# Two-layer graph network on one NeuronCore: the range guard's products on GpSimd, its largest values in one VectorE reduction

## The chip, the cores and the metric

The kernel runs on one NeuronCore of one Trainium2 chip. The core has five engines that work side by side and wait for each other by semaphores: TensorE (PE in the profile, with its weight loads as PEld), VectorE (DVE), ScalarE (ACT), GpSimd (POOL) and SyncE (SP), which here only issues transfers. The metric is the device time of one execution in microseconds, as the median of five runs.

## The reference

The reference takes 3327 nodes with 64 features and a 0/1 adjacency matrix `adj` of 3327 x 3327, and applies two layers, each with a layer norm and a relu ahead of it and a residual sum behind it.

```
h = max(layernorm(x), 0)
x = x + L0(h, adj)          # hyperbolic graph attention
h = max(layernorm(x), 0)
x = x + L1(h, adj)          # sum over the last 100 neighbours, with decay

L0: c = 1/r**2
    att[i,j] = sigmoid(left[i] + right[j] + b) * adj[i,j]
    support[i] = sum_j att[i,j] * logmap(h[i], h[j], c)
    return proj(expmap(h, support, c), c)

L1: rank = cumsum(adj != 0, axis=1)
    w[i,j] = mask * 0.5**(number of later neighbours of i behind j), for the last 100
    return w @ (h @ weight) + bias
```

`logmap` contains an artanh of a distance that depends on both nodes, so it has to be evaluated for each of the 3327 x 3327 pairs. The kernel's fast version replaces that function of the pair by a fit made of two Gelu evaluations, which is good only while the largest feature norms lie in a certain range. A range guard finds the largest values of three per-node quantities and sets a flag; if the flag is set, a slow general version runs after the fast one. With the inputs of this case it does not.

## The kernel before

Nodes are padded to 26 blocks of 128. The 26 blocks j lie on the partitions in turn, and the nodes i lie along the free axis in four strips of 8, 8, 6 and 4 blocks (`STRIPS`). A round handles one block j (two in the last strip) against one strip: 26 + 26 + 26 + 13 = 91 rounds, numbered n from 0. Each round has the same steps, on tiles of 128 x 1024 (128 x 768 in the third strip):

- SyncE loads a part of the adjacency into `ad` (L616), four rounds ahead of its use, into one of five buffers.
- VectorE turns it into a 0/1 `mask` (L622, `edges`), two rounds ahead.
- TensorE counts the later neighbours into PSUM (L633, L634), and ScalarE or VectorE in turn writes the counts to SBUF (L656 and L660 or L658, `read`). They are kept in `behind_lo`, `behind_hi` and `weight_of` for the second layer.
- TensorE makes the pair distance `pq` (L688, L689, `products`), in one of two PSUM buffers.
- ScalarE evaluates the tanh of the attention into `sg` (L671, `sigmoids`), and two Gelus on `pq`, one after the other in place (L881, `gelu`).
- VectorE forms `(tanh + 1) * ad` (L676, `pair_one`) and `(pq + WD) * sg` (L681, `pair_two`).
- TensorE sums over j (L701, `total`).

Around the rounds lie a set-up (layer norm, the per-node scalars `x2`, `bal`, `nrm` and others from L736 to L802 on VectorE, features in L805 on VectorE and from L820 on ScalarE, transposes on TensorE), and after each strip a stage of small per-node steps (`post`), which runs inside the next strip's rounds, mostly on GpSimd. After the last strip, the second layer multiplies the kept counts' weights with the features (L1269) and transposes back (L1429).

For TensorE, VectorE and ScalarE the program's text fixes the order of instructions (`manual_schedule` with `IN_ORDER`). GpSimd and SyncE are not in that set: the framework's scheduler orders what is issued on them by when it can run, so an instruction can stand in their queues far ahead of where the text has it. On GpSimd the set-up puts, among others, a copy of `x2` (the first strip's `dots`, L1078), `ih` (L963), six DMAs that turn `iu` and `iz` into parts of `ju` and `jz` (L867), the products `hw` (L919), and `su` and `sv` (L964, L965).

The change touches the guard's first part, `range_steps` (L978 to L990). It reads `nrm`, `x2`, `bal` and the constant `node` (0 for padding nodes), all 128 x 26, and writes the four columns of `st`: the largest `nrm`, the largest `c * x2 * nrm`, the largest `bal`, and the largest of `-bal`. It is a generator: `advance` runs it piece by piece between the steps of rounds, and each `yield` names the size of the piece. `PORTIONS[0] = 2` allows two units in each round of the first strip, and the first call of `advance` is in round n = 4, so the four pieces with `yield 2` between them run in the rounds n = 4, 5, 6 and 7, which are the fifth to the eighth. In each, they stand on VectorE right after L681. The guard's second part (`in_range`, L992 to L1009) reads `st` near the end of the rounds.

`post_pool`, where the guard's work tile lies, is allocated in SBUF ahead of the pools `strip` and `work`, whose tiles follow it.

Of the kernel before, what the change touches and what calls it, by code (L numbers as in the profile page):

```python
# [12 lines left out]
F32 = mybir.dt.float32  # L13
# [6 lines left out]
ALU = mybir.AluOpType  # L20
AX = mybir.AxisListType
PSUM = bass.MemoryType.PSUM

P = 128
N = 3327
NB = 26
# [13 lines left out]
BIG, LATER, ACT, POOL = 4, 99, 100, 101  # L40
# [408 lines left out]
def fast(ctx, tc, x, adj_t, r, w_att, b_att, weight, bias, out, flag):  # L449

    nc = tc.nc
    V, A, G, T = nc.vector, nc.scalar, nc.gpsimd, nc.tensor
# [47 lines left out]
    node = const.tile([P, NB], F32, name="node")  # L500
# [4 lines left out]
    def scalar_col(name):  # L505
        return const.tile([P, 1], F32, name=name)

    inv_r, c_c, sqc, absr, maxnorm, c2_c, m2c, p2c, negc, zs_c, za_c, f_c = (
        scalar_col(n) for n in ("inv_r", "c_c", "sqc", "absr", "maxnorm", "c2_c", "m2c", "p2c", "negc", "zs_c", "za_c",
                                "f_c"))  # L510
# [15 lines left out]
    def wide(t, n):  # L526
# [3 lines left out]
    x2, bal, balm, nrm, left, right, sv, su, sk, ih = (  # L530
        const.tile([P, NB], F32, name=n)
        for n in ("x2", "bal", "balm", "nrm", "left", "right", "sv", "su", "sk", "ih"))
# [10 lines left out]
    post_pool = ctx.enter_context(tc.tile_pool(name="post", bufs=1))  # L543
    st = const.tile([P, 4], F32, name="st")
# [431 lines left out]


    def range_steps():  # L978
        t1 = post_pool.tile([P, NB], F32, name="st1")
        V.tensor_mul(t1, nrm, node)  # L980
        V.tensor_reduce(st[:, 0:1], t1, AX.X, ALU.max)
        yield 2
        V.scalar_tensor_tensor(t1, x2, c_c, t1, op0=ALU.mult, op1=ALU.mult)
        V.tensor_reduce(st[:, 1:2], t1, AX.X, ALU.max)
        yield 2
        V.tensor_mul(t1, bal, node)
        V.tensor_reduce(st[:, 2:3], t1, AX.X, ALU.max)
        yield 2
        V.tensor_reduce(st[:, 3:4], t1, AX.X, ALU.min)
        V.tensor_scalar(st[:, 3:4], st[:, 3:4], -1.0, None, op0=ALU.mult)  # L990

    def in_range():  # L992
        pf = ps.tile([P, P], F32, name="pc")
# [270 lines left out]
    def add(j, wt, n):  # L1264
# [5 lines left out]
                 start=j == order[0], stop=j == NB - 1)  # L1270

    stages, rest_of_ahead = [Stage(range_steps())], last_of_ahead()
    range_end = in_range()
    load(LOADS)
# [225 lines left out]
```

## Time and profile before

| | us |
|---|---|
| median of 5 runs | 398.43 (397.96 to 399.12) |
| the profiled execution | 397.54 |
| its span, from the first instruction to the last | 395.8 |
| set-up, until ScalarE's row of L656 at 43.34 | 43.3 |
| rounds of the strips one to three | 43.3 to 288 |
| last strip, last `post`, second layer, output | 288 to 395.8 |

The granted TensorE clock has a mean of 0.992 in this execution. In 40 equal slices, of 9.9 us each (busy share in tenths, 9 for 90% or more), two engines and GpSimd read:

```
DVE  4999999999999999999999999999998999798941
ACT  3589999999999999999999999999988899697510
POOL 8145200000000166842133674951246678234100
```

In the timeline each line has the start in us, the duration in us (of all, where several are merged as "x2"), the engine, the line in the kernel, the operation, the tiles written and read with their shapes, and in brackets the idle time of the engine ahead of it with what ended it. A list of waits has the waiting instruction, the one that released it, and the sum, the number and the longest of these waits. Buffer numbers are left out of tile names, and some names are cut at a digit: the guard's `st1` appears as `st`, `x2` as `x`, `q0_c` as `q_c`. The chain of waits is followed back from the last instruction: at each step to what released it, or to the instruction ahead of it on its engine.

### The profile page before, as it was taken

What the parts mean: (1) busy time and instruction counts of PE and PEld (TensorE: products, weight loads), DVE (VectorE), ACT (ScalarE), POOL (GpSimd) and SP (SyncE); (2) the same over time, 40 slices, a digit from 0 to 9 for tenths busy, and PEclk for the clock granted to TensorE, in tenths of its full rate; (3) what the DMA queues carried; (4) which work ended last, traced back from release to release, by engine and by line L of the source; (5) the groups of instructions that cost most, each with busy time, mean ns of one, the idle gap of its engine ahead of it and who ended that gap; (6) DMA issues with size and microseconds to landing.
All of it is one profiled execution on the core that took longest, in us unless ns stands there. A gap on an engine that the chain in (4) does not pass through costs nothing.

```text
span 395.8 us, 4776 instructions
## 1 busy us (share of the span) xinstructions
PE 350.1 (88%) x1460; PEld 149.3 (38%) x1460; DVE 363.6 (92%) x551; ACT 348.5 (88%) x401; POOL 143.1 (36%) x279
## 2 busy tenths in 40 slices
PE   0077999999999899999998999999987899999892
PEld 0053333333333333333333344444433333344362
DVE  4999999999999999999999999999998999798941
ACT  3589999999999999999999999999988899697510
POOL 8145200000000166842133674951246678234100
PEclk9999999999999999999999999999999999999996
DMA  7314554454557445545444445554654330000022
GB/s 205 153 43 135 174 155 147 132 159 153 159 159 221 130 148 159 159 135 162 133 129 135 132 140 161 144 142 154 189 155 133 109 106 0 2 0 1 2 48 48
DMA packets 23299, 49.00 MB, mean 124 GB/s; under 512 B 8789, under 2 KB 9245, under 8 KB 23265
## 3 DMA queue, kind: packets, MB, share of 16 engines
q1 hardware_dynamic: 20993, 47.66, 39.8%
q10 hardware_dynamic: 1808, 0.46, 0.7%
q0 software_dynamic: 464, 0.49, 0.5%
q8 instruction: 13, 0.21, 0.2%
q14 instruction: 21, 0.17, 0.1%
HBM read 46.40 MB, written 0.87 MB: 119 GB/s over the span
## 4 chain that ended last, share of the span: by engine, by line
DVE 42%; ACT 27%; issue 15%; PE 12%; POOL 2%; DMA 1%; POOLq 0%; DVEq 0%; ACTq 0%
DVE sg L681 12%; DVE sg L676 12%; ACT pq L881 10%; ACT sg L671 7%; PE po L701 4%; DVE mask L622 3%; ACT behind_hi L656 2%; ACT behind_lo L656 2%; DVE behind_hi L660 1%; PE pc L633 1%; DMA x_sb<-in_x 1%; DVE behind_lo L660 1%; PE pc L634 1%; PE pw L1269 1%; PE pw L1429 1%
## 5 line engine op out<-in xcount | busy, mean ns | idle before, releaser
L881 ACT ACTIVATE pq<-pq 128x1024 f32<-128x1024 f32 (+1 forms) x182 | 174.2, 963 | 2.6 <-PE pq L689 0.8
L701 PE MATMUL po<-sg,hw 128*65 128x512 f32 (+1 forms) x364 | 159.6, 562 | 0.1
L681 DVE SCALAR_TENSOR_TENSOR sg<-pq,sg 128x1024 f32<-128x1024 f32 (+1 forms) x91 | 103.6, 1138 | 3.1 <-ACT pq L881 2.4
L676 DVE SCALAR_TENSOR_TENSOR sg<-sg,ad 128x1024 f32<-128x1024 f32 (+1 forms) x91 | 104.8, 1152 | 0.1
L671 ACT ACTIVATE sg<-left_b,right 128x1024 f32<-128x1024 f32 (+2 forms) x103 | 102.0, 991 | 0.0
L701 PEld LDWEIGHTS po<-sg,hw 128*65 128x65 f32 x364 | 48.9, 137 | 67.1 <-issue 52.9
L633 PE MATMUL pc<-mask,ca 128*128 128x512 bf16 (+1 forms) x175 | 63.5, 363 | 8.4 <-ACT behind_hi L656 4.1
L688 PE MATMUL pq<-iu,ju 71*128 71x512 f16 (+1 forms) x182 | 66.5, 366 | 1.1 <-ACT jz L818 0.8
L634 PE MATMUL pc<-mask,cb 128*128 128x512 bf16 (+1 forms) x182 | 64.6, 365 | 1.7 <-DVE mask L622 1.0
L689 PE MATMUL pq<-iz,jz 128*128 128x512 f16 (+1 forms) x182 | 65.0, 364 | 0.0
L622 DVE TENSOR_SCALAR mask<-ad 128x1024 bf16<-128x1024 f32 (+1 forms) x91 | 59.1, 650 | 0.0
L634 PEld LDWEIGHTS <-cb 128*128 128x128 bf16 x182 | 17.7, 97 | 47.1 <-issue 34.3
L1108 POOL CAST w<-mask 128x1 f32<-128x1 bf16 x3 | 1.5, 504 | 89.3 <-ACT sg L671 89.2
L633 PEld LDWEIGHTS <-ca 128*128 128x128 bf16 x175 | 17.1, 98 | 30.5 <-issue 18.3
L688 PEld LDWEIGHTS <-ju 71*128 71x128 f16 x182 | 17.8, 98 | 23.1 <-DVE sg L681 5.5
L1269 PEld LDWEIGHTS <-s 128*128 128x128 f16 x182 | 17.7, 98 | 21.3 <-DVE s L1093 2.3
L689 PEld LDWEIGHTS <-jz 128*128 128x128 f16 x182 | 17.9, 98 | 18.6 <-issue 1.1
L660 DVE TENSOR_SCALAR behind_lo<-pc 128x1024 uint8<-128x1024 f32 (+2 forms) x24 | 24.4, 1017 | 0.3 <-PE pc L634 0.3
L656 ACT ACTIVATE behind_hi<-pc 128x1024 uint8<-128x1024 f32 (+2 forms) x25 | 21.9, 874 | 1.3 <-PE pc L634 1.3
L656 ACT ACTIVATE behind_lo<-pc 128x1024 uint8<-128x1024 f32 (+2 forms) x24 | 20.9, 871 | 0.0
L852 PE MATMUL pq<-id,nui 128*71 128x128 f16 x8 | 1.0, 311 | 20.9 <-ACT nzi L826 20.9
L660 DVE TENSOR_SCALAR behind_hi<-pc 128x1024 uint8<-128x1024 f32 (+2 forms) x15 | 14.8, 985 | 0.9 <-PE pc L634 0.7
(344 smaller groups left out, 382.4 us busy)
## 6 DMA issues: line engine op xcount, KB each, us to landing
ad<-in_adj_t SPq DMA_DIRECT2D x65, 512.0 KB, 3.5
ad<-in_adj_t SPq DMA_DIRECT2D x26, 384.0 KB, 3.1
out<-o SPq DMA_DIRECT2D x6, 128.0 KB, 1.9
left_b<-left_d SPq DMA_DIRECT2D x1, 512.0 KB, 4.2
x_sb<-in_x SPq DMA_DIRECT2D x1, 416.0 KB, 4.8
x_sb<-in_x ACTq DMA_DIRECT2D x1, 416.0 KB
left_b<-left_d SPq DMA_DIRECT2D x1, 384.0 KB
jz<-iz POOLq DMA_DIRECT2D x2, 128.0 KB, 2.6
```

Of the source, the lines that this page charges most:

```text
L622: V.tensor_scalar(*args, 0.0, None, op0=ALU.not_equal)
L633: T.matmul(S.pc[:, f0:f1], ca, S.before[:, f0:f1], start=False, stop=True, skip_group_check=True)
L634: T.matmul(S.pc[:, f0:f1], cb, now[:, f0:f1], start=S.first, stop=True, skip_group_check=True)
L656: A.activation(kept, of, AF.Relu, scale=128.0 if j in JD else 1.0)
L660: V.tensor_scalar(kept, S.pc[:, : S.F], 0.0, None, op0=ALU.max)
L671: A.activation(part(n, sg, j), S.left[:, : S.F], AF.Tanh, bias=right[:, j : j + 1], scale=0.5)
L676: V.scalar_tensor_tensor(sg, sg, 1.0, ad_of.pop(n)[:, :w], op0=ALU.add, op1=ALU.mult)
L681: V.scalar_tensor_tensor(sg, pq_of.pop(n)[:, :w], WD, sg, op0=ALU.add, op1=ALU.mult)
L688: T.matmul(part(n, pq, j, f0, f1), ju[:KB, j, :], S.iu[:, f0:f1], start=True, stop=False)
L689: T.matmul(part(n, pq, j, f0, f1), jz[:, j, :], S.iz[:, f0:f1], start=False, stop=True)
L701: T.matmul(po[: D + 1, : f1 - f0], hw[:, j, :], part(n, sg_of[n], j, f0, f1), start=j == NB - 1, stop=j == 0)
L881: A.activation(pq, pq, AF.Gelu, scale=scale)
```

## The change

The four pieces become two. The first issues five instructions on GpSimd, which write the four products into the four rows of one tile `tops` (128 x 4 x 26): `nrm * node`, `c * x2` times that row, `bal * node`, and minus that row. The second is one VectorE reduction over the last axis, which writes all four columns of `st` at once. `yield LATER` ends a round's share, so in the text the products stand in the round n = 4 and the reduction in n = 5. Eight VectorE instructions become one, and GpSimd gets five more. The work tile grows from 104 to 416 bytes per partition, and in the built program the tiles that lie behind it in `post_pool`, `strip` and `work` move by 288 bytes per partition. The last column was the least `bal` times -1, and is now the largest of `-bal`, which is the same number.

```
     def range_steps():
-        t1 = post_pool.tile([P, NB], F32, name="st1")
-        V.tensor_mul(t1, nrm, node)
-        V.tensor_reduce(st[:, 0:1], t1, AX.X, ALU.max)
-        yield 2
-        V.scalar_tensor_tensor(t1, x2, c_c, t1, op0=ALU.mult, op1=ALU.mult)
-        V.tensor_reduce(st[:, 1:2], t1, AX.X, ALU.max)
-        yield 2
-        V.tensor_mul(t1, bal, node)
-        V.tensor_reduce(st[:, 2:3], t1, AX.X, ALU.max)
-        yield 2
-        V.tensor_reduce(st[:, 3:4], t1, AX.X, ALU.min)
-        V.tensor_scalar(st[:, 3:4], st[:, 3:4], -1.0, None, op0=ALU.mult)
+        tops = post_pool.tile([P, 4, NB], F32, name="tops")
+        G.tensor_mul(tops[:, 0], nrm, node)
+        G.tensor_scalar(tops[:, 1], x2, c_c, None, op0=ALU.mult)
+        G.tensor_mul(tops[:, 1], tops[:, 1], tops[:, 0])
+        G.tensor_mul(tops[:, 2], bal, node)
+        G.tensor_scalar(tops[:, 3], tops[:, 2], -1.0, None, op0=ALU.mult)
+        yield LATER
+        V.tensor_reduce(st, tops, AX.X, ALU.max)
+        yield LATER
```

## The prediction, made before the result was known

> **What bounds the kernel now.** I read the page first (busy shares, then the chain), then the busy time by stage, then ScalarE's waits, then the timeline of VectorE and ScalarE around the steps that the change removes. On the page VectorE is the busiest engine and has the largest share of the chain:
>
> ```profile
> PE 350.1 (88%) x1460; PEld 149.3 (38%) x1460; DVE 363.6 (92%) x551; ACT 348.5 (88%) x401; POOL 143.1 (36%) x279
> DVE 42%; ACT 27%; issue 15%; PE 12%; POOL 2%; DMA 1%; POOLq 0%; DVEq 0%; ACTq 0%
> ```
>
> So work taken from VectorE looks like time won. By stage the answer is closer (columns: stretch, its length, then busy time of PE, PEld, DVE, ACT, POOL; the three rows are the strips one, two and three):
>
> ```profile
> 43.34:127.50 84.16, 83.24 (x286) 31.28 (x285) 83.35 (x93) 83.40 (x86) 1.77 (x2) 1.00 0.53 161
> 127.50:213.00 85.50, 84.11 (x297) 32.20 (x296) 84.83 (x89) 84.74 (x90) 36.10 (x68) 1.00 0.48 147
> 213.00:288.00 75.00, 71.56 (x321) 33.40 (x320) 73.89 (x99) 74.80 (x103) 38.71 (x74) 1.00 0.51 150
> ```
>
> VectorE and ScalarE are both full. What remains of ScalarE's time is 0.03 us ahead of each second L881, which rewrites the first one's tile. Which of the two sets the pace is shown by who waits. ScalarE's waits from 44 to 288 us are one entry, and that is the one that ends at 43.34:
>
> ```profile
> ACT behind_hi L656 <- PE pc L634: 0.3, 1, 0.3
> ```
>
> For 245 us ScalarE waits for nobody, and nothing taken from VectorE inside that stretch can bring a ScalarE instruction forward. The timeline shows where VectorE stands behind it:
>
> ```profile
> 49.55 1.22 DVE L681 SCALAR_TENSOR_TENSOR sg<-pq,sg 128x1024 f32<-128x1024 f32 x1
> 50.68 0.18 DVE L980 TENSOR_TENSOR st<-nrm,node 128x26 f32<-128x26 f32 x1
> 50.90 0.18 DVE L981 TENSOR_REDUCE st<-st 128x1 f32<-128x26 f32 x1
> 50.99 1.22 DVE L676 SCALAR_TENSOR_TENSOR sg<-sg,ad 128x1024 f32<-128x1024 f32 x1
> ...
> 71.95 2.06 ACT L881 ACTIVATE pq<-pq 128x1024 f32<-128x1024 f32 x2
> 75.41 1.21 DVE L681 SCALAR_TENSOR_TENSOR sg<-pq,sg 128x1024 f32<-128x1024 f32 x1
> ...
> 150.34 2.06 ACT L881 ACTIVATE pq<-pq 128x1024 f32<-128x1024 f32 x2
> 152.78 1.22 DVE L681 SCALAR_TENSOR_TENSOR sg<-pq,sg 128x1024 f32<-128x1024 f32 x1
> ```
>
> Take the distance from the end of a round's second L881 to the start of its L681. Before the small steps, L881 ends at 47.27 + 2.05 = 49.32 and L681 starts at 49.55: 0.23. After them it is 75.41 - 74.01 = 1.40. At 152.78 it is 0.38 (150.34 + 2.06 = 152.40), and in the next round, where L881 ends at 155.41 and L681 starts at 155.64, 0.23 again. VectorE falls about a microsecond behind because of the small steps, makes it up by about 150 us, and no instruction of ScalarE shows either. That memory ends there; whatever the small steps did is gone 245 us before the end.
>
> **The removed steps.** VectorE's cost is read from start to start, since its instructions overlap. Without small steps L676 starts 1.13 after L681 (46.68 to 47.81). With them: 50.99 - 49.55 = 1.44, 55.36 - 53.86 = 1.50, 58.53 - 57.10 = 1.43, 62.81 - 61.40 = 1.41. The excess is 0.31 + 0.37 + 0.30 + 0.28 = 1.26 us over four rounds.
>
> **The one reduction added.** No row has 128x104. Bounds: 0.18 (128x26, L981) and four of them, 0.72. Between L981 and L743 (128x832, 1.02 us) the slope is 0.84 / 806 = 1.04 ns per element, so 0.18 + 78 x 1.04 ns = 0.26 us, which I take. VectorE saves about 1.26 - 0.26 = 1.0 us (0.5 to 1.1). On the path to the end I count 0: ScalarE's own row covers it. If that cover were missing, the gain would be 1.0.
>
> **The wait added.** The reduction waits for GpSimd. Behind it stand L676 of round 6 and everything after on VectorE. In the built program's order the five products do not stand where they are written, about 50 us in. They go to the front of GpSimd's queue, between and after the two instructions that the set-up has there, as soon as x2, bal and nrm exist, and ahead of the six DMAs of L867:
>
> ```profile
> 17.51 0.19 POOL L1078 COPY dots<-x 128x8 f32<-128x8 f32 x1 [1.53 <-DVE x L792]
> 18.04 0.32 POOL L963 TENSOR_SCALAR ih<-babs 128x26 f32<-128x26 f32 x1 [0.34 <-DVE babs L796]
> 24.29 0.60 POOL L867 DMA_DIRECT2D ju<-iu  x1 [5.93 <-DVE yr L872]
> ```
>
> Prices: three products of two tiles at 0.24 (L964, 128x26) and two by a constant at 0.32 (L963): 1.36, about 1.6 us with the 0.3 from start to start that L964 and L965 show. GpSimd is then done near 20, against 24.29 for the first DMA: 4 us of the 5.93 idle remain. The reduction stands near 54 and never waits. Cost 0; the DMAs of L867 would be late only if the products took over four times their rows.
>
> **What the products do to VectorE's set-up.** This is the one place where the path is touched. From 17.03 to 18.72 the chain of waits runs through VectorE's L790 to L801 and then to ScalarE's first L820. What is lost there arrives at the end in full. Rows on both sides: from 15.19 to 15.97 GpSimd runs four single-column instructions without a break (L967 to L970), and VectorE's two-operand steps beside them keep their time (L519 0.21, L521 0.23, against 0.21 alone at 16.29 and 16.54). Against that, a large one:
>
> ```profile
> 134.59 1.28 POOL L1109 TENSOR_TENSOR w<-hw,agg 128x512 f32<-128x512 f32 x1
> 135.30 1.65 DVE L676 SCALAR_TENSOR_TENSOR sg<-sg,ad 128x1024 f32<-128x1024 f32 x1
> ```
>
> 1.65 instead of 1.21: 0.44 lost beside 1.28. Our tiles have 26 columns, nearer to one column than to 512. By the small rows the loss is 0 to 0.02 for each of five products, and I take 0.1 in all. The upper bound: L796, L797 and L800, the three two-operand steps of the chain after x2, are each held for one whole product of 0.32, 0.96 us. Below nothing it can't go: nothing on the chain is removed there. Products that fall after 18.8 meet L805, whose reader L825 starts on ScalarE at 19.81 behind four instructions of its own, so a few tenths there are free.
>
> [...]
>
> **SyncE.** The products also shift the load order near 120 us: the third strip's left_b (L583), which today waits 4.3 us for ScalarE in the queue, goes behind that strip's iu loads, and one load of ad behind two iz loads and one iu load. The ad load issued at 121.86 is first read by the mask at 133.56, and loads there land in at most 5.8 us: 5.9 spare. The earlier one, at 120.08, is read at 128.63: 2.8 spare, and it loses the wait ahead of it. left_b is read at 215. Cost 0.
>
> **Sum.** The profiled execution took 397.54 (span 395.8, 1.7 around it). 397.54 + 0 (VectorE) + 0 (wait) + 0.1 (set-up) + 0 (loads) = 397.64. The profile lies 0.89 below the runs' median of 398.43, so on the runs' scale 398.5.
>
> **The rivals.**
> Saving arrives (faster): VectorE is what sets the pace, and 1.0 us reaches the end: 397.4. For it: 92%, 42% of the chain, and the chain does run through VectorE from 46.68 to 69.8. Against it: the chain changes to ScalarE at 70, where ScalarE had already been without a gap since 43.34. 12%.
> GpSimd in VectorE's way (slower): during 17.5 to 18.7 the products hold the chain's steps; at the bound 399.4. It decides from about 0.8 us. For it: L676 at 135.30. Against it: the rows at 15.2 to 16. 15%.
> A load too late (slower): through the new order, or because the larger tile moves all work tiles behind it in SBUF and loads get slower. A load would have to take 2.8 us more than 5.8; then ScalarE's reading of counts would stall, about 1 us: 399.4. 3%.
> The change not doing what it says, with products late and the reduction waiting: it needs GpSimd to be 34 us later than I place it. Within the rest.
>
> **How the numbers follow.** A measurement here tells from no change about 0.2%, 0.8 us. Forecast, no change: 70%, of which 1% each strays over a bound by measurement alone. Faster 0.12 + 0.01 = 0.13; slower 0.15 + 0.03 + 0.01 = 0.19; same 0.68. Range: from 397.5, next to the saving in full, to 399.4, the bound on the set-up.
>
> **What would show it.** Right: five GpSimd rows between 17.5 and 20; VectorE's L681 after 62 us 0.2 to 0.4 behind L881 instead of 1.4; ScalarE's waits from 44 to 288 empty as before; the first L820 within 0.1 of 18.77. Wrong: an L820 at 19.2 or later, a wait of ScalarE on VectorE or PE in strip one, or a mask that waits for a load.

## The result, and the profile after

The change is slower, by about 1.1 us: 399.61 us as the median of 27 runs (398.38 to 401.29) against 398.50 us for 51 runs of the kernel before beside it, ratio 1.0032 with a 95% interval of 1.0021 to 1.0043. The predicted time was 398.5 us and the range ended at 399.4. The profiled execution took 399.36 us against 397.54, its span is 397.6 us against 395.8.

The medians hide how the runs lie. Those of the change fall into two groups, 14 between 398.38 and 399.61 and 13 between 400.44 and 401.29, with nothing between. The kernel before has most of its runs below 399.7 and 8 of 51 above. Below, "lower runs" are those under 399.7 us and "upper runs" the rest. The line was drawn with the runs in view, and three of the change's later runs fall just above it, between 399.7 and 400.0. With the repeats of both kernels:

| | runs | median | mean of the lower runs | upper runs | mean of the upper runs |
|---|---|---|---|---|---|
| before | 224 | 398.56 | 398.45 | 46 (21%) | 400.12 |
| the change | 49 | 399.67 | 399.01 | 24 (49%) | 400.78 |

So there are two things to explain: 0.55 us in the lower runs, and a share of upper runs that is more than doubled. (A kernel that is slower throughout also gets more runs over a fixed line; but 21 of the 49, or 43%, lie even above a line that is 0.55 us higher.)

The profile after shows first that what was predicted of the engines came about. The page has 7 VectorE instructions fewer, 5 more of GpSimd, and the chain lies less on VectorE:

```profile
PE 352.2 (89%) x1460; PEld 151.5 (38%) x1460; DVE 363.6 (91%) x544; ACT 348.4 (88%) x401; POOL 145.4 (37%) x284
...
PE 30%; DVE 29%; ACT 24%; issue 11%; POOL 2%; DMA 2%; POOLq 0%; SPq 0%; DVEq 0%; ACTq 0%
```

The timeline of the change (start, duration, engine, line, operation, tiles) has the five products early in the set-up and the reduction in the round n = 5; line numbers behind the edit are three lower than before:

```profile
17.40 0.43 POOL L981 TENSOR_SCALAR tops<-x,c_c 128x26 f32<-128x26 f32 x1 [1.57 <-DVE yr L793]
...
17.93 0.25 POOL L983 TENSOR_TENSOR tops<-bal,node 128x26 f32<-128x26 f32 x1
...
18.27 0.33 POOL L984 TENSOR_SCALAR tops<-tops 128x26 f32<-128x26 f32 x1
...
18.63 0.32 ACT L820 ACTIVATE g<-g,one_c 128x27 f32<-128x27 f32 x1 [4.39 <-POOL tops L984]
...
18.68 0.80 POOL L963 TENSOR_SCALAR ih<-babs 128x26 f32<-128x26 f32 x1
...
19.44 0.23 POOL L980 TENSOR_TENSOR tops<-nrm,node 128x26 f32<-128x26 f32 x1
...
19.75 0.32 POOL L982 TENSOR_TENSOR tops<-tops 128x26 f32<-128x26 f32 x1
...
20.59 0.18 DVE L839 COPY nui<-nu 128x24 f16<-128x24 f16 x1
...
24.25 0.61 POOL L867 DMA_DIRECT2D ju<-iu  x1 [4.19 <-DVE yr L872]
...
55.25 0.25 DVE L986 TENSOR_REDUCE st<-tops 128x4 f32<-128x104 f32 x1
...
72.45 2.06 ACT L881 ACTIVATE pq<-pq 128x1024 f32<-128x1024 f32 x2
...
74.89 1.22 DVE L681 SCALAR_TENSOR_TENSOR sg<-pq,sg 128x1024 f32<-128x1024 f32 x1
```

The profile puts the release of L820 down to L984, but L820 doesn't read `tops`; it starts 1.74 us behind the start of L790, as it did before. L881 ends at 74.51 and L681 starts at 74.89: 0.38 us behind, where it stood 1.40 behind before. VectorE's saving is there. ScalarE's waits from 44 us to 289 us, however, are the same single entry as before, with the same 0.3 us:

```profile
ACT behind_hi L656 <- PE pc L634: 0.3, 1, 0.3
```

Nothing of the saving reaches ScalarE. Its start times stand 0.50 us later than before at 43.84, where the rounds begin, and still 0.35 later at 289.

The 1.82 us between the two profiles' spans lie elsewhere, and are found by laying each engine's start times of one over those of the other: +0.50 us by 43.84 (back to +0.35 by 289), +0.5 within one round at 294, +0.47 between the end of the last add of the output (L1431 before, L1428 after) and the end of SyncE's branch behind the flag, +0.33 from that branch to SyncE's next instruction, +0.18 after it. What of this belongs to the change, and what to one execution, only the experiments tell.

### The profile page after: what moved, and what is told of

Same layout as the page of the kernel before. It is cut to its first block, busy times and chain, and to the rows that moved or that the text cites. A ratio compares the mean times of both kernels' runs of the same rounds, so it can differ in the third digit from the quotient of the medians.

```text
span 397.6 us, 4776 instructions
## 1 busy us (share of the span) xinstructions
PE 352.2 (89%) x1460; PEld 151.5 (38%) x1460; DVE 363.6 (91%) x544; ACT 348.4 (88%) x401; POOL 145.4 (37%) x284
## 4 chain that ended last, share of the span: by engine, by line
PE 30%; DVE 29%; ACT 24%; issue 11%; POOL 2%; DMA 2%; POOLq 0%; SPq 0%; DVEq 0%; ACTq 0%
PE po L701 12%; ACT pq L881 9%; DVE sg L676 8%; DVE sg L681 8%; ACT sg L671 5%; PE pc L633 3%; PE pc L634 3%; PE pq L689 3%; PE pq L688 3%; ACT behind_hi L656 3%; DVE mask L622 2%; DVE behind_lo L660 1%; DMA x_sb<-in_x 1%; PE pw L1266 1%; PE pw L1426 1%
## 5 line engine op out<-in xcount | busy, mean ns | idle before, releaser
L881 ACT ACTIVATE pq<-pq 128x1024 f32<-128x1024 f32 (+1 forms) x182 | 173.8, 960 | 2.6 <-PE pq L689 0.8
L681 DVE SCALAR_TENSOR_TENSOR sg<-pq,sg 128x1024 f32<-128x1024 f32 (+1 forms) x91 | 103.7, 1139 | 3.7 <-ACT pq L881 2.8
L676 DVE SCALAR_TENSOR_TENSOR sg<-sg,ad 128x1024 f32<-128x1024 f32 (+1 forms) x91 | 105.2, 1156 | 0.1
L688 PE MATMUL pq<-iu,ju 71*128 71x512 f16 (+1 forms) x182 | 67.0, 368 | 1.1 <-ACT jz L818 0.9
L689 PE MATMUL pq<-iz,jz 128*128 128x512 f16 (+1 forms) x182 | 65.5, 367 | 0.0
L688 PEld LDWEIGHTS <-ju 71*128 71x128 f16 x182 | 17.9, 98 | 21.6 <-DVE sg L681 3.0
L689 PEld LDWEIGHTS <-jz 128*128 128x128 f16 x182 | 18.0, 99 | 19.6 <-issue 1.5
L656 ACT ACTIVATE behind_hi<-pc 128x1024 uint8<-128x1024 f32 (+2 forms) x25 | 21.8, 873 | 1.5 <-PE pc L634 1.5
L656 ACT ACTIVATE behind_lo<-pc 128x1024 uint8<-128x1024 f32 (+2 forms) x24 | 20.8, 867 | 0.0
```

Of the source, the lines that this page charges most:

```text
L656: A.activation(kept, of, AF.Relu, scale=128.0 if j in JD else 1.0)
L676: V.scalar_tensor_tensor(sg, sg, 1.0, ad_of.pop(n)[:, :w], op0=ALU.add, op1=ALU.mult)
L681: V.scalar_tensor_tensor(sg, pq_of.pop(n)[:, :w], WD, sg, op0=ALU.add, op1=ALU.mult)
L688: T.matmul(part(n, pq, j, f0, f1), ju[:KB, j, :], S.iu[:, f0:f1], start=True, stop=False)
L689: T.matmul(part(n, pq, j, f0, f1), jz[:, j, :], S.iz[:, f0:f1], start=False, stop=True)
L881: A.activation(pq, pq, AF.Gelu, scale=scale)
```

## The experiments

The theories at the start. P: the products on GpSimd cost time in the set-up. V: taking VectorE's steps out, with the changed load order, costs time. A: the larger tile moves the tiles behind it, by 288 bytes, and that costs time. C: TensorE's clock, which differs from one profile to the other (recorded at full speed from 23.94 us in the one before and from 29.96 us in the one after, and at half from 389.16 and 391.77), makes the difference by chance. Each kernel has a median over 10 to 12 runs, and a ratio to 23 to 35 runs of the kernel before on the same chip. "Moved" tiles are given by their address modulo 512 bytes: 0 before, 288 after.

**The change again, and its parts alone**

r1_again is the change, unchanged.

> The changed kernel once more. Theory C (the extra time is where TensorE's clock rises and falls, which is chance): times spread over the same modes as the kernel before, and the ratio comes out anywhere from 0.998 to 1.003; in the profile the rise to full clock may lie at 24 us or at 30 us whatever the kernel. Theories P (products on GpSimd), V (VectorE's steps gone and loads in a new order) and A (addresses): the ratio is again 1.002 to 1.004.

Measured: 399.60 us, ratio 1.0029 (1.0010 to 1.0048), lower runs 399.06, 4 of 10 upper. The effect is real and repeats.

r1_both adds the products but keeps the eight VectorE steps and the load order of before:

```
     def range_steps():
+        tops = post_pool.tile([P, 4, NB], F32, name="tops")
+        G.tensor_mul(tops[:, 0], nrm, node)
...
+        G.tensor_scalar(tops[:, 3], tops[:, 2], -1.0, None, op0=ALU.mult)
         t1 = post_pool.tile([P, NB], F32, name="st1")
```

> The five products on GpSimd are added, but the eight VectorE steps of before stay and write st (the products are read by nobody); the load order on SyncE is that of before. P: all of the loss, about +1.2 us (ratio 1.003). V: none, within 0.3 us. A: about +1.2 (the tiles are moved here too, by 416 bytes). C: within 0.5 us of before, either side.

Measured: 398.84 us, 1.0019 (1.0000 to 1.0038), lower runs 398.55, 5 of 12 upper. Its moved tiles lie at 416.

r1_no_steps leaves both the steps and the products out, so that the guard's four values are not computed; tiles at 288 and load order are those of the change:

```
         tops = post_pool.tile([P, 4, NB], F32, name="tops")
-        G.tensor_mul(tops[:, 0], nrm, node)
...
-        V.tensor_reduce(st, tops, AX.X, ALU.max)
+        V.memset(st, 0.0)
```

> Neither the eight VectorE steps nor the products: st is set to 0 by one memset, so the guard's largest values are left out. The load order on SyncE is that of the changed kernel, tiles are moved by 288 bytes as there. V: about +1.2 us although only work is taken away. P: no loss, within 0.3 us. A: about +1.2. C: within 0.5 us of before, either side.

Measured: 399.22 us, 1.0023 (1.0010 to 1.0037), lower runs 398.98, 4 of 12 upper.

r1_wide_tile is the kernel before with a larger work tile and nothing else:

```
-        t1 = post_pool.tile([P, NB], F32, name="st1")
+        t1 = post_pool.tile([P, 4, NB], F32, name="st1")[:, 0]
```

> The kernel before with its guard tile enlarged to the size of the new one, so that the tiles behind it move by 288 bytes and nothing else differs. A: about +1.2 us. P and V: none, within 0.3 us. C: within 0.5 us, either side.

Measured: 399.17 us, 1.0012 (0.9997 to 1.0027), lower runs 399.01, 2 of 12 upper. The interval just takes in 1, but the lower runs stand where those of the change stand: 399.01 with the same instructions as before in the same order. This points to A for the lower runs. V falls: r1_no_steps, without VectorE's steps, and r1_wide_tile, with all eight, have the same addresses and the same lower runs, 398.98 and 399.01, so these runs show no gain and no loss from the steps.

**One profile against another: a coincidence at 293 us**

The +0.5 at 294 us looked like the whole answer. The timeline there, first of the kernel before, then of the change:

```profile
293.34 1.82 POOL L1392 TENSOR_TENSOR x_sb<-x_sb,bias_b 128x256 f32<-128x256 f32 x1
...
293.36 1.22 DVE L676 SCALAR_TENSOR_TENSOR sg<-sg,ad 128x1024 f32<-128x1024 f32 x1
```

```profile
293.68 0.72 POOL L1389 TENSOR_TENSOR x_sb<-x_sb,bias_b 128x256 f32<-128x256 f32 x1
...
293.70 1.79 DVE L676 SCALAR_TENSOR_TENSOR sg<-sg,ad 128x1024 f32<-128x1024 f32 x1
```

GpSimd's bias add and VectorE's L676 start within some 20 ns of each other, and one of them holds the other up: GpSimd takes 1.82 us and VectorE 1.22, or GpSimd 0.72 and VectorE 1.79. Everything behind is 0.5 us later in the second case. All five profiles with moved tiles showed the second, the one profile without moved tiles the first. So the kernel before was profiled once more:

> The kernel before, unchanged, for a second profile. Theory A (the larger tile moves the work tiles, and that alone turns round the meeting near 293.4 us of GpSimd's bias add L1392 and VectorE's L676): L676 there takes 1.22 us again and the add 1.82. Theory T (that meeting is a tie that either side can win in any kernel, as the two start within 20 ns): about one chance in two of L676 1.79 and the add 0.73, with 0.55 us more of everything behind. Theory P (products in the set-up) says nothing here. Time by all: ratio 1.000, few runs (about 1 in 7) at 400 or more.

Measured: 398.44 us, 1.0005 (0.9989 to 1.0022), 3 of 12 upper, and the meeting goes the other way:

```profile
293.44 0.72 POOL L1392 TENSOR_TENSOR x_sb<-x_sb,bias_b 128x256 f32<-128x256 f32 x1
...
293.47 1.78 DVE L676 SCALAR_TENSOR_TENSOR sg<-sg,ad 128x1024 f32<-128x1024 f32 x1
```

Of the 20 profiles of this study VectorE came first in 3: one of the two of the kernel before, one of the three of the change, and one of r3_o_home. GpSimd's start is recorded first in all 20, by 15 to 25 ns, and by 15 or 16 in the three. It is a tie that differs from execution to execution, and not the change. One more of the five differences goes the same way: from SyncE's branch to its next instruction it takes 2.45 to 2.89 us, in no relation to the kernel.

The +0.50 at 43.84 fits TensorE's clock, which reached full speed 23.94 us after the start in the profile before and 29.96 us in the one after, where L689 takes 0.63 us at 25.06 and 0.38 at 32.02. From the first matmul to the third L656 it takes 19.98 to 20.00 us in the seven profiles in which the clock rose before 25 us, and 20.44 to 20.53 in the seven in which it rose 8.8 to 9.4 us behind the first matmul (the one with an extra matmul, below, left out). r5_count, which has the change's products and addresses, was profiled with a rise at 24.23, so the change does not force the late one. Whether it makes the late one likelier stays open: the clock rose at 28.6 us or later in 8 of the 9 profiles with the products in the set-up and in 5 of the 11 without.

**The same tiles, moved by 512 bytes**

r2_wide_512 enlarges the tile of the kernel before so that the moved tiles lie at 0 again:

```
-        t1 = post_pool.tile([P, NB], F32, name="st1")
+        t1 = post_pool.tile([P, 160], F32, name="st1")[:, :NB]
```

> Before, with the guard's work tile enlarged by 512 bytes instead of 288, nothing else. Theory A in its form 'address within 512 bytes matters': as before, L676 near 293.4 us 1.22, ratio 1.000. Theory A in its form 'any move matters': L676 1.79, +0.4 to 0.5 us, ratio 1.001. Theory T: either, and a ratio that is the same as that of the wide tile within its interval. Runs at 400 or more: 1 in 7, as there are no products in the set-up.

Measured: 398.40 us, 0.9998 (0.9979 to 1.0016), lower runs 398.44, 2 of 12 upper. Not the move, but where it ends, costs here: 399.01 with the same tiles at 288 in r1_wide_tile.

r2_aligned and r3_aligned are the change with a fill, so that the tiles lie at 0 (run twice, the second time for the share of upper runs):

```
         tops = post_pool.tile([P, 4, NB], F32, name="tops")
+        post_pool.tile([P, 56], F32, name="fill")
```

> The change whole, plus a fill tile of 224 bytes, so that the tiles behind move by 512 bytes instead of 288. Theory A (512 bytes matter): L676 near 293.4 us 1.22 and the add 1.82, about 0.5 us less than the change, 399.0. Theory P (products in the set-up make a run at half TensorE clock near 40 us likelier): runs at 400 or more stay at 4 in 10. Theory T: L676 1.22 or 1.79, and the time as that of the change, 399.5.

> The change plus the fill of 224 bytes ahead of all moved tiles, run once more for the share of its runs at 399.7 or more, which was 1 of 12. Theory P (products): 4 in 10 or more, 13 of 27 as in the change. Theory A': 1 in 6 or fewer, as all addresses are on multiples of 512 as before. The lower runs at 398.5 by theory O.

Measured: 398.72 us, 0.9994 (0.9979 to 1.0008), 1 of 12 upper; then 398.99 us, 1.0003 (0.9984 to 1.0022), 4 of 12. Together the lower runs have a mean of 398.59, 0.42 below those of the change. The part of the expectation about 293 us fell with the tie: GpSimd came first in both.

**The products later**

r2_late holds the products back on GpSimd by four copies of one column each from a mask that exists late; they then stand behind the set-up:

```
         tops = post_pool.tile([P, 4, NB], F32, name="tops")
+        for row in range(4):
+            G.tensor_copy(tops[:, row, :1], mask_of[4][:, :1])
         G.tensor_mul(tops[:, 0], nrm, node)
```

> The change with its five products held back on GpSimd: four copies of one column from a mask row that exists late make them stand behind su and sv, out of the set-up's chain. Theory P: the share of runs at 400 or more falls from 4 in 10 to 1 in 7, and the median falls to 399.0. Theory C (the clock dip comes by chance in each kernel alike): about 1 in 4 in this one and in the aligned one. Theory A: L676 near 293.4 us 1.79, since the tiles move by 288 bytes. VectorE's L801 to L839 and PE's L852 start as before, within 0.05 us of one another's shift.

Measured: 399.11 us, 1.0012 (0.9994 to 1.0029), lower runs 398.99, 4 of 12 upper. The set-up shows the products' own price. From the start of ScalarE's first L820 to VectorE's L839 the change takes 18.63 to 20.59, which is 1.96 us; the kernel before takes 1.85, and so does r2_late:

```profile
18.77 0.32 ACT L820 ACTIVATE g<-g,one_c 128x27 f32<-128x27 f32 x1 [4.38 <-DVE g L801]
...
20.62 0.18 DVE L839 COPY nui<-nu 128x24 f16<-128x24 f16 x1
```

(before), and

```profile
18.94 0.32 ACT L820 ACTIVATE g<-g,one_c 128x27 f32<-128x27 f32 x1 [4.34 <-DVE g L801]
...
20.79 0.18 DVE L839 COPY nui<-nu 128x24 f16<-128x24 f16 x1
```

(r2_late). The products in the set-up cost 0.11 us, in every profile that has them there. In the lower runs this is within what the runs can tell.

**What reads the moved tiles: the output**

With the tiles at 0 and at 288, one view differs in every profile, the list of transfers (tiles, queue, count, size, median us from issue to landing). Before, then the change:

```profile
out<-o SPq DMA_DIRECT2D x6, 128.0 KB, 1.9
...
out<-o SPq DMA_DIRECT2D x1, 32.0 KB, 2.6
```

```profile
out<-o SPq DMA_DIRECT2D x6, 128.0 KB, 2.1
...
out<-o SPq DMA_DIRECT2D x1, 32.0 KB, 2.8
```

The second output transfer lands 1.91 to 1.93 us after its issue in all ten profiles with `o` at 0, 2.05 us with `o` at 416, and 2.06 to 2.08 us in all nine at 288. At the very end this counts: the general version's flag is read by SyncE behind the last output transfer, and that read, the branch on it, and the end of the program stand in line (SyncE's rows before: the last transfer's issue at 389.57 to 390.02, the read at 390.07 to 390.92, the branch at 390.99 to 391.03). From the end of the last add to the end of SyncE's branch (SyncE's own rows, which the timeline leaves out):

```
o at 0:    2.51 before   2.51 before, again   2.50 aligned   2.51 aligned, 2nd   1.71 wide_512
o at 416:  2.76 both
o at 288:  2.97 change   2.97 again   2.84 wide_tile   3.00 no_steps   2.98 late
```

(In wide_512, and in r3_x_home below, the last transfer was issued 0.47 us behind the one ahead of it; elsewhere that gap is 0.8 to 1.3 us. Why isn't known.) Two kernels test whether `o` alone does it. r3_o_moved is the kernel before with only `o` moved, to 288; r3_o_home is the change with only `o` moved back, to 0, by 56 in place of 72 in the same line:

```
                    for q in range(4)]
+        l1.tile([P, 72], F32, name="fill", bufs=1)
```

> The kernel before, with a fill tile of 288 bytes ahead of the four output tiles o and nothing else moved. Theory O (what costs is that the output transfers read from o at an address 288 bytes off a multiple of 512): the second output transfer lands 2.07 us after its issue instead of 1.92, from the end of the last add L1431 to SyncE's branch behind the flag 2.97 us instead of 2.50, the runs below 399.7 have a mean of 399.0 instead of 398.45. Theory A (any of the other tiles that move): 1.92, 2.50 and 398.45 as before. The share of runs at 399.7 or more stays near 1 in 6 by theory P, as there are no products in the set-up.

> The change, with a fill tile of 224 bytes ahead of o, so that o lies on a multiple of 512 bytes again while the other moved tiles stay 288 bytes off. Theory O: 1.92, 2.50 us, the lower runs at 398.5 instead of 399.07. Theory A: 2.07, 2.97, 399.07. Theory P (products in the set-up): 4 in 10 of the runs at 399.7 or more; theory A' (addresses make those runs likelier): 4 in 10 too; chance: 1 in 6.

```profile
out<-o SPq DMA_DIRECT2D x6, 128.0 KB, 2.1
```

(r3_o_moved), and

```profile
out<-o SPq DMA_DIRECT2D x6, 128.0 KB, 1.9
```

(r3_o_home). Measured: in r3_o_moved the second transfer takes 2.08 us and the stretch to the branch 3.05; in r3_o_home 1.92 and 2.50. The times follow in part. r3_o_moved: 398.76 us, 1.0007 (0.9989 to 1.0026), lower runs 398.70, 0.25 above the kernel before. r3_o_home: 398.90 us, 0.9998 (0.9983 to 1.0014), lower runs 398.73, 0.28 below the change. So the output tiles are shown to cost 0.5 us of the end in the profiles; how 0.15 us of a transfer becomes 0.5 at the end isn't shown. In the lower runs they cost 0.25 and 0.28 us, about half of the 0.55, each uncertain by 0.1 to 0.2, and the interval of r3_o_moved's ratio takes in 1. If a rest remains, it lies elsewhere. One more place is seen, though not tried alone: the set-up's transfers from `iz` to `jz` land after 2.55 to 2.60 us in all profiles in which the other moved tiles lie at 0, and 2.61 to 2.71 in all nine in which they lie at 288.

**Fewer instructions, a later end**

The last 0.18 us of the two profiles' difference is no chance either. In all nine profiles of kernels without VectorE's eight steps (the change, no_steps, late, aligned, o_home, after_fill) VectorE's last DRAIN, at the end of the program, stands 0.48 us behind the instruction ahead of it, and from SyncE's first instruction behind the branch to the end of the span it is 2.41 us. In the nine with the steps (before, both, wide_tile, wide_512, o_moved, x_home, x_fill) it stands 0.09 behind, and the end takes 2.23. r5_count gives the change its number of VectorE instructions back; r5_all_back takes out the three costs found, the address (fill of 224 bytes), the products in the set-up (the four copies of r2_late) and the number:

```
         yield LATER
+        for _ in range(7):
+            V.memset(st, 0.0)
         V.tensor_reduce(st, tops, AX.X, ALU.max)
```

> The change plus seven small VectorE memsets of st just ahead of the reduction, so that VectorE has as many instructions as before. In all nine profiles of kernels without the eight steps VectorE's last instruction stands 0.48 us behind the one ahead of it, and the span ends 0.18 us later; in all nine with as many instructions as before it stands 0.09 behind. Theory I (the number of VectorE's instructions does it, by where the last one lies): 0.09 again, 2.23 us from SyncE's first instruction behind the branch to the end instead of 2.41. Rival (the load order of the change, or the missing steps themselves, do it): 0.48 and 2.41. The memsets cost 0 to 0.1 us on the path, as VectorE's 1 us of saving covers them. Lower runs 398.8 by I, 399.0 by the rival.

> The change with all three known costs taken out: tiles on multiples of 512 bytes (fill of 224 bytes), products held back behind the set-up, seven VectorE memsets for the count. If the costs found are all there is: lower runs at 398.46 as in the kernel before (0.1 each way), second output transfer 1.92 us, L820 to L839 1.85 us, VectorE's last instruction 0.09 behind; upper runs 1 in 5. If something else of the change costs, lower runs at 398.7 or more.

Measured: in both 0.09 and 2.23 us, so it goes with the number of VectorE's instructions and not with which they are; what hangs on it there was not tried. r5_count: 399.45 us, 1.0023 (1.0004 to 1.0042), lower runs 398.95, which can't tell 0.18 us. r5_all_back: 398.69 us, 1.0002 (0.9984 to 1.0020), lower runs 398.58 (uncertain by 0.2), 1 of 12 upper, second output transfer 1.93 us, L820 to L839 1.85 us. With the three costs gone the change stands where the kernel before stands, as far as these runs can tell. VectorE's saving is gone there too: the seven memsets take 0.85 us, and from L681 to L676 around them and the reduction it is 2.30 us instead of 1.13. What tells that the saving is worth nothing is r1_no_steps beside r1_wide_tile.

**The upper runs: TensorE's clock**

In r1_again, r2_aligned, r3_o_home and r3_x_home the granted clock of TensorE falls to half for 3.4 us at 39 to 43 us; in no other profile does it fall there (in r2_late and r5_all_back it falls at 31.6 to 35.0). The stretches around it in r1_again (from and to, length, then busy time of PE, PEld, DVE, ACT, POOL with their instructions, granted clock, share and rate of transfers):

```profile
36.57:39.98 3.41, 2.10 (x24) 1.16 (x24) 2.79 (x7) 3.17 (x5) 0.00 (x0) 1.00 0.76 227
39.98:43.40 3.42, 3.20 (x7) 1.22 (x7) 3.38 (x6) 3.39 (x4) 0.01 (x1) 0.50 0.45 103
43.40:46.81 3.41, 3.23 (x12) 1.16 (x11) 2.19 (x3) 1.38 (x3) 1.89 (x4) 1.00 0.81 287
```

The change's profile, without the fall, and r1_again, with it, have ScalarE's fourth L656 at:

```profile
43.84 1.02 ACT L656 ACTIVATE behind_hi<-pc 128x1024 uint8<-128x1024 f32 x1 [0.35 <-PE pc L634]
```

```profile
45.79 1.02 ACT L656 ACTIVATE behind_hi<-pc 128x1024 uint8<-128x1024 f32 x1 [2.03 <-PE pc L634]
```

From the first matmul to this L656 it takes 24.04 to 24.25 us in the four profiles with the fall, 22.84 to 22.93 in the seven with a late rise and no fall, and 22.38 to 22.40 in the seven with an early rise, those with the fall at 31.6 among them: the fall at 39 to 43 costs 1.1 to 1.9 us, the one at 31.6 nothing here, and the upper runs of the change stand 1.77 above its lower ones. Of the 51 runs of the change for which a mean clock is listed, 18 of the 21 at 400.3 or more have 0.985 or 0.986, and one of the other 30.

In these profiles a fall goes with the time from the first matmul to the rise. In the 18 profiles without an extra matmul, ordered by that time: 2.9 to 3.3 us, no fall (5 profiles); 3.65 and 3.80, a fall at 31.6 (2); 7.8 to 8.2, a fall at 39 to 43 (4); 8.8 to 9.4, no fall (7). The change, its aligned form and x_home (below) each stand in both of the last two groups, so the same program falls in one execution and not in the next.

In r1_again TensorE was busy for 2.10 of 3.41 us, and then ran 3.42 us at half clock, where a matmul of L688 takes 0.64 us instead of 0.38. In the change's own profile the stretch ahead, 36.79 to 40.20, has 2.46 us busy, and no fall follows. The hole is 0.91 us ahead of L895, which waits for ScalarE's L818. In r1_no_steps, r3_o_moved and r5_count the stretch with this hole has 2.08 us busy, and no fall follows either, so the busy time alone does not decide. r4_after_fill puts one matmul more into it, whose result the next one overwrites:

```
+    T.matmul(bank(0)[: D + 1, :], hw[:, NB - 1, :], part(0, sg_of[0], NB - 1, 0, 512), start=True, stop=True)
     total(0)
     logits((low,), p5[:, : 2 * NB].rearrange("p (b c) -> p b c", c=2))
```

> The change plus one matmul of 128x512 more on TensorE near 36.5 us, ahead of the first total(0), whose result is overwritten: it fills a hole of 0.92 us in which TensorE waits for ScalarE's L818. Theory G (the runs at 399.7 or more are those whose TensorE clock falls to half for 3.4 us near 40 us, because TensorE was busy for only 0.62 of the 3.4 us before): the busy share of that stretch rises to about 0.85, no run shows the half clock there, no run is at 400.3 or more, and the median falls to 399.1. Theory N (the upper runs have another cause): 4 of 12 runs at 400.3 or more, as without the matmul.

> The change once more, unchanged, beside the kernel with the matmul. Theory P or A' (the change itself makes upper runs likelier): again 4 to 5 in 10 at 400.3 or more, where it had 17 of 37. Theory C (chance): the share falls towards the 1 in 4 of the other kernels.

Measured: the change again, 399.81 us, 1.0021 (1.0003 to 1.0039), with 4 of 12 runs at 400.3 or more. With the matmul 399.13 us, 1.0003 (0.9987 to 1.0019), all of its 12 runs between 398.72 and 399.74. The change without it had 21 of 49 runs at 400.3 or more. By the line at 399.7 it is 2 of 12 against 24 of 49, and the profiled one of these two had no fall. In its profile the two stretches ahead of 41.06 are filled and the clock holds:

```profile
34.23:37.65 3.42, 3.36 (x29) 1.54 (x25) 3.26 (x7) 3.39 (x4) 2.49 (x2) 1.00 0.51 144
37.65:41.06 3.41, 3.01 (x28) 1.51 (x27) 2.80 (x8) 3.12 (x4) 0.00 (x0) 1.00 0.75 212
41.06:44.47 3.41, 3.41 (x13) 1.33 (x12) 3.25 (x6) 3.07 (x4) 0.54 (x3) 1.00 0.66 134
```

This profile alone shows little, as its clock rose 9.3 us behind the first matmul, where none fell without the matmul either. The other one with the matmul, x_fill of the next part, rose at 8.5, nearer to those that fell; beside r2_aligned, which rose at 7.8 (first), it has the stretch filled and no fall:

```profile
35.72:39.13 3.41, 2.10 (x23) 1.07 (x23) 2.72 (x8) 3.17 (x5) 0.02 (x1) 1.00 0.81 212
39.13:42.55 3.42, 3.42 (x9) 1.30 (x8) 3.42 (x5) 3.39 (x4) 0.00 (x0) 0.50 0.51 90
```

```profile
35.77:39.18 3.41, 3.01 (x27) 1.41 (x26) 2.80 (x7) 3.12 (x4) 0.00 (x0) 1.00 0.77 233
39.18:42.60 3.42, 3.42 (x14) 1.29 (x13) 3.39 (x6) 3.39 (x4) 0.11 (x1) 1.00 0.49 87
```

Theory G fits: runs at 400.3 or more come with the half clock in this hole, and with the matmul there are none. That no run with it had the half clock anywhere can't be said. One of the 12 has a mean clock of 0.986, as the upper runs have, and took 399.72; and 7 of the 12 of x_fill have 0.986 or 0.987 and took 0.85 us longer on average than the other five. None of these was profiled.

Why the change has so many upper runs is not settled. Upper runs by kernel: 21% before, 28% of 36 with tiles at 288 but no products in the set-up, 21% of 24 with products and tiles at 0, 5 of 12 in r1_both, 4 of 12 in r3_o_home, 5 of 12 in r5_count, 49% of 49 in the change. Neither part alone gives the share. All four falls at 39 to 43 us are in profiles with the late rise; if the products make the late rise likelier, that would be the link, but it is argued and not shown.

**A version that beats both**

What the output showed (1.92 us with `o` at 0, 2.07 at 288) can be tried where a move is free. The input tile `x_sb`, which the whole set-up waits for, lies at 160:

```
+    const.tile([P, 88], F32, name="fill")
     x_sb = const.tile([P, NB, D], F32, name="x_sb")
+    const.tile([P, 40], F32, name="fill2")
```

> The kernel before with the input tile x_sb moved from 160 bytes past a multiple of 512 to a multiple of 512, and the tiles behind it by 512. A try to use theory O: if reading and writing off 512 bytes costs a transfer time in general, the first half of x lands 0.1 to 0.4 us earlier than 5.63 to 5.83 after the start, and the runs are at 398.1 to 398.4. If it costs only transfers that read from SBUF: 398.5, as before.

> The kernel before with x_sb on a multiple of 512 bytes, once more, beside the one with the matmul, to tell the two apart. As before: first half of x in at 5.2 us, lower runs at 397.9, upper runs at 399.0 to 399.5, median 398.0 to 398.6 by the share of the upper ones.

> The kernel before, with x_sb on a multiple of 512 bytes and the extra matmul near 36.5 us: the version that should beat both. Theory G: no upper runs (399.0 and more), so a median at 397.9 instead of 398.55 for x_sb alone; ratio to before 0.998. Theory N: about half of its runs at 399.0 or more, median 398.5.

Measured: x_home, on the kernel before, 398.55 us, 0.9986 (0.9968 to 1.0003), then 397.88 us, 0.9976 (0.9957 to 0.9995); x_fill, with the extra matmul too, 398.12 us, 0.9981 (0.9964 to 0.9998). VectorE's first use of `x_sb`, before and in r4_x_home:

```profile
5.65 1.02 DVE L736 TENSOR_REDUCE m<-x_sb 128x13 f32<-128x832 f32 x1 [5.65 <-DMA x_sb<-in_x]
```

```profile
5.29 1.02 DVE L738 TENSOR_REDUCE m<-x_sb 128x13 f32<-128x832 f32 x1 [5.29 <-DMA x_sb<-in_x]
```

The three profiles with `x_sb` at 0 have this row at 5.16 to 5.29, the other 17 at 5.50 to 6.07. The matmul's part: 6 of the 24 runs of x_home and none of the 12 of x_fill are at 399.0 or more, but by the medians (398.03 over all of x_home, 398.12) the two are not told apart. Against the kernel before, x_fill and one of the two measurements of x_home are faster beyond their intervals; both have medians about 1.6 us below that of the change.

## Why the prediction was wrong

- **What bounds the kernel, and the removed steps: right.** VectorE's distance behind ScalarE after 62 us fell from 1.40 to 0.38 us, and ScalarE's waits stayed as they were. The saving counts 0 on the path, as said.
- **The one reduction: right**, 0.25 us against 0.26.
- **The wait added: right.** The products stand at 17.40 to 20.07, ahead of the first L867 at 24.25; the reduction at 55.25 has its data for 35 us. One transfer of L867 was touched: the sixth lands after 2.14 to 2.49 us instead of 1.72 to 1.74 in the profiles with products there, with nothing seen to wait for it.
- **What the products do to VectorE's set-up: right in size, off in place.** 0.11 us against 0.1, far from the upper bound of 0.96. The first L820 is not late; the loss lies between L820 and L839, where the prediction had counted products behind 18.8 us as free. Its sign of being wrong, an L820 at 19.2 or later, tells nothing: L820 stands at 19.25 or 19.26 in six profiles, three of them without products, in all of which the first load landed late (`x_sb` first used at 5.90 to 6.07 us). No run shows the hold that the bound assumes, a whole product for each of three steps: L796, L797 and L800 take 0.19, 0.18 and 0.25 us in the profile after, as before. Beside L805, which keeps its 0.68, it was GpSimd's `ih` that took longer: 0.80 us instead of 0.32.
- **SyncE: right** as far as ScalarE shows it; no wait of ScalarE from 44 to 289 us.
- **The sum: here it failed.** It has terms for instructions only, and none for the tile's size. That the work tiles move by 288 bytes stood beside it, but was priced in the rival "a load too late" at 3%, for the loads of `ad` alone, which have 2.8 us to spare. The transfers with nothing to spare are those at the end: the output tiles lie among the moved ones, and from the last add to the branch 2.51 us became 2.97. The lower runs put 0.55 us on the change, of which these tiles alone brought 0.25 to 0.28, and with all moved tiles back at 0 the change gained 0.42. Nor has the sum a term for the number of VectorE's instructions, which the profiles put at 0.18 us of the end.
- **The step from the profile to the runs' scale: the second failure.** "The profile lies 0.89 below the runs' median" was taken as a constant. The runs are two groups, 1.7 us apart, and a constant holds only while their shares do. The five runs shown before, all under 399.2, had none of the upper group. With the share of before, 21%, the change's mean would have been 399.01 + 0.21 x 1.77 = 399.38 us; it was 399.88. So the share brought 0.5 us of this mean, nearly as much as all the rest; where it comes from stays open.
- **The rivals.** "Saving arrives" and "GpSimd in VectorE's way" both fell. "A load too late through the larger tile" named the address, which the runs show, and the wrong transfer.

On the first failure: the output goes in packets of 256 bytes, 1024 of them in the second transfer, and that transfer landed after 1.92 us with `o` at 0, 2.05 at 416 and 2.07 at 288. The page of the kernel before has `o` at 0 alone, so it gives no time for another address, and the packets themselves are not recorded as longer (16 ns on average at 288, 18 at 0).

## What to carry to other kernels

When a change alters the size of a tile, list the tiles behind it and what transfers read or write them, and price the new address first for the transfers that nothing covers, here the first input and the last output. Pad so that such tiles start where they did; here a fill tile of 224 bytes was worth 0.4 us of the change's lower runs. And before a difference of two profiles is explained, profile the kernel before a second time: a tie between two engines that shows 0.5 us in one pair of profiles may be chance.

## What the runs showed of the hardware that was not expected

- A fall of TensorE's clock to half lasted 3.41 or 3.42 us, and came 6.83 or 10.24 us behind the rise. The rise lay between 23.9 and 30.8 us after the start, and differed by 1.1 to 1.2 us between two executions of one kernel (28.89 and 29.95 in aligned, 28.59 and 29.79 in x_home). Ahead of the falls TensorE was busy for about 2.10 us of 3.41 four times, and for 1.58 and 1.63 once each, while other stretches with as little, such as 1.58 in r3_o_moved, were followed by none. What decides was not shown.
- The place of a tile went with a few tenths of a microsecond: 0.15 us of a 128 KB transfer out of SBUF (1.92 with `o` at 0, 2.07 at 288), and at least 0.2 us of the first load into `x_sb` (first used at 5.16 to 5.29 us with `x_sb` at 0, at 5.50 to 6.07 at 160).
- The recorded packets of the slower output transfers are the shorter ones, 16 ns on average with `o` at 288 against 18 ns at 0 and 416; the later landing is not in the packets' own times. No run explains that.
- With seven VectorE instructions fewer, VectorE's last DRAIN stood 0.39 us later (0.48 against 0.09 us behind the instruction ahead of it) and the end came 0.18 us later (2.41 against 2.23), in every one of 20 profiles.
- GpSimd's bias add and VectorE's L676 beside it (293 us in the profile before) started within 25 ns of each other in all 20 profiles, and it went either way: L676 took 1.79 us instead of 1.22 beside the add of 0.72 (17 profiles), and the add 1.82 beside L676 at 1.22 (3).
